# Layer 0's sum over 16 terms: a tree of additions in place of one strided reduction

## The chip, the core and the metric

The kernel runs on one core of a Trainium2 chip. The metric is the device time of one launch in microseconds. The core has five engines with a queue each, which run in parallel and wait for each other by semaphores: TensorE (PE, matrix products into PSUM; its weight loads are shown apart, as PEld), VectorE (DVE), ScalarE (ACT), GpSimd (POOL) and SyncE (SP); the last two mostly issue DMA transfers here.

## The reference

Four graph layers are applied in turn to x of 8 batches, 2048 nodes and 64 channels, with one 2048 x 2048 adjacency matrix `adj`. Each is a residual with a layer norm:

```python
x = _layernorm(x + L0(x, adj, embedding, weight, bias))   # graph convolution, weights per node
x = _layernorm(x + L1(x, adj, a))                         # attention
x = _layernorm(x + L2(x, adj, W, b))                      # mean over neighbours
x = _layernorm(x + L3(x, adj, iv, W1, b1, W2, b2))        # three message steps
```

Layer 0 is where the change lies. With K = 3 hops and D = 16 embedding entries per node:

```python
w = jnp.einsum('nd,dkio->nkio', embedding, weight)        # a weight matrix per node
As = [I, A, 2 A @ A - I]
x_g = jnp.einsum('knm,bmc->bnkc', jnp.stack(As), x)
out = jnp.einsum('bnki,nkio->bno', x_g, w) + embedding @ bias
```

The weight matrix of node n is a sum of 16 matrices, weighted with the 16 entries of its embedding. So the output of a node is a sum of 16 terms: x_g times matrix d, times embedding[n, d].

## The kernel before

**Tiling.** A tile has 128 nodes on the partitions; there are 16 node tiles. The 8 batches are taken as 4 pairs p, so that a tile of x is 128 nodes by 2 batches by 64 channels = 128x128, and `SX[p]` holds the 16 tiles of a pair. All data are fp32 (masks in DRAM are bf16). The adjacency matrix streams from DRAM in tiles of 512 KB (`a`), 6 of them in flight, through SP's queue in one fixed order (`order_of_a`, `fetch`).

**Layer 0.** `first_product` and `second_product` (the matmuls `acc`, line 1094) form A x and A (A x). Then `second_pass` makes, for each node tile, the products with all 16 matrices: 16 x 128 values per node come in two halves of 8 matrices, each half in a PSUM tile `yp` of 128 x 2 x 512 (line 601). `add_terms` takes a half from PSUM into the SBUF tile `terms` of 128 x 16 x 128, scaled with the node's embedding entry: 8 small ACT instructions per half (line 624). For pair 0 (`shared`) the second half is done by DVE instead, which adds its 8 terms onto the 8 of the first half (line 627), so that 8 terms are left. After the second half DVE sums what is in `terms` (16 terms, or 8 for pair 0) with one reduction into `added` (line 636) and adds that to the pair's tile `v` of `SX` (line 639). There are 64 such sums, 16 per pair: 16 of 8 terms and 48 of 16. When the four tiles of a chunk are done, `first_norm` and `layer_norm` follow (lines 482 to 510, 650).

**Layer 1.** `scores` finds each row's maximum with DVE (`junk`, line 732, 128x2048), and `weights` makes the attention weights `e` of 128x2048 in four steps: DVE adds a mask (line 810), ACT applies a leaky slope (line 818), DVE adds the negative maximum (line 823), ACT exponentiates (line 826). PE sums neighbours with them (`po`, line 837), and `finish` divides and adds.

**Layers 2 and 3.** They run on PE for pairs 0 and 1 as further sweeps over the adjacency matrix (also line 1094), with small products between them (`ps_u`, `ps_v`, lines 1029 and 1049). Pairs 2 and 3 are done jointly at the end (`joint_layer2`, line 1213, and `joint_layer3`, line 1300), with sums of adjacency quarters that are stored and read back (`s`, line 1173).

**What sets the order.** Every instruction's place in its engine's queue is fixed when the program is built. A planner (`Plan`) holds the generators of all this work as threads. Each thread names the engine that it wants next and what must be done before. The planner starts the thread that could begin earliest by its own clock, and `plan.run` advances that clock by a price that the code gives: `dve(n)` = n / 960 + 0.07 us, `act(n)` = n / 1220 + 0.14 us, and so on. Hence the price given for an instruction decides what is placed around it, on all engines, for the rest of the program; the adjacency sweeps (rank 1000) fill what is left of PE. Buffers are `Ring`s, which the planner also gives back at planned times; `terms` and the attention weights `e` share one of 4 buffers (`e_ring`).

For the sum of 16 terms the price before is `dve(2048) + dve(128) + 0.1` = 2.51 us, for that of 8 terms `dve(1024) + dve(128) + 0.1` = 1.44 us.

Of the kernel before, what the change touches and what calls it, by code (L numbers as in the profile page):

```python
# [12 lines left out]
ALU = mybir.AluOpType  # L13
AX = mybir.AxisListType
# [3 lines left out]
P = 128  # L18
# [10 lines left out]
D0 = 16  # L29
# [105 lines left out]
def dve(n, k=1):  # L135
    return k * (n / 960 + 0.07)
# [7 lines left out]
def resnorm_d4_kernel(  # L144
# [21 lines left out]
    nc = tc.nc  # L166
    plan = Plan()
# [28 lines left out]
    def tiny(shape, name, bufs=4):  # L196
        return wp.tile(shape, F32, tag=name, name=name, bufs=bufs)
# [7 lines left out]
    def batches(v):  # L205

        if len(v.shape) == 3:
            v = v.rearrange("p t n -> p (t n)")
        return v.rearrange("p (b c) -> p b c", c=C)
# [366 lines left out]
    def second_pass():  # L576

        for n in range(NPAIR * NCH):
# [4 lines left out]
            for j in range(TPC):  # L583
                t = c * TPC + j
                cs = slice(j * P, (j + 1) * P)
                for h in range(2):
                    hs = slice(h * CW, (h + 1) * CW)

                    ring = pp_ring
                    if p == 0 and po_ring.ready() < pp_ring.ready():  # L590
                        ring = po_ring
                    if h == 0 or ring.ready() > plan.free["PE"]:
                        yield "PE", [("xg", n + 1), got, ring, *([e_ring] if h == 0 else [])]
                    if h == 0:
                        terms = e_ring.take([P, D0, P], "terms")
                    yp, k = ring.take([P, 2, CW], "yp")

                    for k2 in (h, 1 - h):
                        for e in range(2):
                            rows = slice(e * C, (e + 1) * C) if k2 else slice(0, P)  # L600
                            nc.tensor.matmul(  # L601
                                yp[:, e, :],
                                lhsT=y2T[rows, cs] if k2 else xg[:, e, cs],
                                rhs=(wk2 if k2 else w01)[rows, hs],
                                start=(k2 == h),
                                stop=(k2 != h),
                            )
                    t_pe = plan.run("PE", 2.8, got)
                    plan.start((2, 2, 1, 1)[p], add_terms(p, c, t, h, yp, ring, k, terms, t_pe, left))
# [3 lines left out]
    def add_terms(p, c, t, h, yp, ring, k, terms, t_pe, left):  # L613

        shared = p == 0
        eng = "DVE" if shared and h else "ACT"
        yield eng, [t_pe, *([("terms", p, t)] if shared and h else [])]
        v = SX[p][:, t, :]
        for d in range(8):
            dd = h * 8 + d  # L620
            term = yp[:, :, d * C : (d + 1) * C]
            weight = emb_sb[:, t, dd : dd + 1]
            if eng == "ACT":
                nc.scalar.activation(batches(terms[0][:, dd, :]), term, AF.Copy, scale=weight)  # L624
            else:
                to = batches(terms[0][:, d, :])
                nc.vector.scalar_tensor_tensor(to, term, weight, to, ALU.mult, ALU.add)
        done = plan.run(eng, 8 * (0.255 if eng == "ACT" else 0.29), t_pe)
        ring.give(k, done)
        if h == 0:  # L630
            at["terms", p, t] = done
            return
        yield "DVE", [done]
        n = 8 if shared else D0
        added = tiny([P, P], "added", 1)
        nc.vector.tensor_reduce(  # L636
            added, terms[0][:, 0:n, :].rearrange("p d n -> p n d"), AX.X, ALU.add
        )
        nc.vector.tensor_tensor(v, v, added, ALU.add)
        done = plan.run("DVE", dve(n * P) + dve(P) + 0.1, done)  # L640
        e_ring.give(terms[1], done)
        left[0] -= 1
        if left[0] == 0:
            plan.start(2, first_norm(p, c, plan.free["DVE"] + plan.LAG))

    def first_norm(p, c, done):
        yield "DVE", [done]
        v = SX[p][:, tiles(c), :]
        v4 = v.rearrange("p t (e c) -> p t e c", c=C)
        nc.vector.tensor_tensor(  # L650
            v4, v4, eb[:, tiles(c), :].unsqueeze(2).to_broadcast([P, TPC, 2, C]), ALU.add
        )
        done = plan.run("DVE", dve(CW), done)
        done = yield from layer_norm(v, CW, done)
        at["n0", p, c] = done
        if all(("n0", p, i) in at for i in range(NCH)):
            at["x1", p] = max(at["n0", p, i] for i in range(NCH))
# [821 lines left out]
```

## Time and profile before

| | |
|---|---|
| median of 3 runs | 2170.16 us (2167.12 to 2171.02) |
| the profiled execution | 2166.21 us, span 2164.4 us |
| mean granted TensorE clock | 0.991 |
| busy: PE, DVE, ACT, POOL | 2081.7, 1552.5, 977.9, 213.6 us |
| sums of 16 terms (line 636) | 48, 3694 ns each, 177.3 us |
| sums of 8 terms (line 636) | 16, 1916 ns each, 30.7 us |
| additions onto x (line 639) | 64, 292 ns each, 18.7 us |
| first sum starts, last addition starts | 159.8 us, 1032.5 us |

The profile is of one execution. "Busy" is the time in which an engine has an instruction at work; a matmul's end is modelled, and matmuls overlap, so that PE's busy time overstates its load. An fp32 matmul of the program is two records in the trace. A wait is put down to the instruction that released it ("<-"), and the chain of waits follows the work that ended last back to its start. The times in a view are from the start of the span.

### The profile page before, as it was taken

The page shows a single profiled execution, that of the slowest core. Times are in us where ns is not written, and L with a number is a line of the kernel's source. Part 1 is how long each engine was busy: PE and PEld are TensorE (multiplying, and loading weights), DVE is VectorE, ACT ScalarE, POOL GpSimd, SP SyncE. Part 2 cuts the span into 40 slices and gives each one's busy share as a digit, 9 for nine tenths or more (in the row PEclk, how much of TensorE's full clock was granted, in tenths as well). Part 3 has the DMA queues.
Part 4 walks back from the last instruction along what each step waited for, and adds up shares of the span by engine and source line. Part 5 has one row for each costly group of instructions (what it writes and reads, how often), then busy time and mean ns, then how long its engine had stood idle before and what let it go on. Part 6 is the DMA issues. An engine that isn't in the chain of part 4 may idle for free.

```text
span 2164.4 us, 18851 instructions
## 1 busy us (share of the span) xinstructions
PE 2081.7 (96%) x6325; PEld 917.0 (42%) x6325; DVE 1552.5 (72%) x1727; ACT 977.9 (45%) x1799; POOL 213.6 (10%) x374
## 2 busy tenths in 40 slices
PE   8999999899999999999999999999999899999998
PEld 3444344334333343333444454443444344444444
DVE  2227648998899999879999979999697455020214
ACT  0025424367776556767653757516676022000002
POOL 2310000101010110110001011010010110000000
PEclk9999999999999999999999999999999999999999
DMA  9899835634353364543669778788776667878785
GB/s 300 268 335 345 290 105 197 218 102 127 90 170 125 116 211 160 180 156 122 232 239 371 232 250 323 250 320 300 247 252 234 231 249 271 283 249 283 252 290 187
DMA packets 208739, 495.84 MB, mean 229 GB/s; under 512 B 20275, under 2 KB 28595, under 8 KB 204531
## 3 DMA queue, kind: packets, MB, share of 16 engines
q1 hardware_dynamic: 165058, 347.62, 47.2%
q0 software_dynamic: 39360, 144.92, 19.6%
q10 hardware_dynamic: 4224, 2.10, 0.4%
q8 instruction: 50, 0.82, 0.1%
q14 instruction: 47, 0.38, 0.1%
HBM read 446.14 MB, written 46.33 MB: 228 GB/s over the span
## 4 chain that ended last, share of the span: by engine, by line
PE 40%; DVE 26%; issue 25%; ACT 5%; DMA 3%; POOL 1%; POOLq 0%; ACTq 0%; SPq 0%; DVEq 0%
PE acc L1094 26%; DVE added L636 8%; PE po L837 6%; DVE junk L732 5%; DVE e L810 5%; PE yp L601 5%; DVE e L823 4%; ACT terms L624 2%; DMA a<-in_adj_t 2%; ACT e L818 1%; PE ps_u L1029 1%; PE acc L1083 1%; POOL s L1175 1%; ACT e L826 1%; DVE ln_v L495 1%
## 5 line engine op out<-in xcount | busy, mean ns | idle before, releaser
L1094 PE MATMUL acc<-a,SX 128*128 128x512 f32 x1024 | 467.3, 600 | 10.9 <-DMA SX<-in_x 6.6
L1094 PE MATMUL acc<-a,SA 128*128 128x512 f32 x768 | 352.5, 600 | 6.9 <-DMA a<-in_adj_t 6.2
L818 ACT ACTIVATE e<-e,sv 128x1024 f32<-128x1024 f32 x256 | 279.5, 1147 | 162.8 <-DVE e L810 161.6
L823 DVE TENSOR_TENSOR e<-e,mb 128x2048 f32<-128x2048 f32 x128 | 290.7, 2284 | 12.7 <-ACT e L818 12.0
L1094 PEld LDWEIGHTS acc<-a,SX 128*128 128x128 f32 x1024 | 191.5, 192 | 253.4 <-issue 237.7
L732 DVE CUSTOM_DVE_ANT_0 junk<-s2b,mr 128x2048 bf16<-128x2048 f32 x128 | 292.5, 2285 | 1.8 <-DMA mr<-by_row 0.5
L810 DVE TENSOR_TENSOR e<-s1b,mk 128x2048 f32<-128x2048 f32 x128 | 289.3, 2283 | 0.9 <-DMA mk<-by_col 0.6
L826 ACT ACTIVATE e<-e 128x2048 f32<-128x2048 f32 x128 | 245.1, 1919 | 92.8 <-DVE e L823 92.4
L624 ACT ACTIVATE terms<-yp,emb_sb 128x128 f32<-128x128 f32 x896 | 242.2, 394 | 78.5 <-PE yp L601 78.3
L601 PE MATMUL yp<-SH,xgT 128*128 128x512 f32 x512 | 248.9, 611 | 7.2 <-ACT terms L624 3.6
L636 DVE TENSOR_REDUCE added<-terms 128x128 f32<-128x2048 f32 (+1 forms) x64 | 208.0, 3249 | 47.7 <-ACT terms L624 47.5
L837 PE MATMUL po<-e,SX 128*64 128x512 f32 x1024 | 235.9, 602 | 2.2 <-ACT e L826 2.2
L1094 PEld LDWEIGHTS acc<-a,SA 128*128 128x128 f32 x768 | 141.1, 191 | 177.7 <-issue 166.1
L1300 PE MATMUL acc<-a,t 128*128 128x512 f32 x384 | 168.7, 592 | 0.0
L601 PEld LDWEIGHTS yp<-SH,xgT 128*128 128x128 f32 x512 | 91.3, 190 | 150.2 <-issue 133.6
L601 PE MATMUL yp<-SH,y2T 64*128 64x512 f32 x512 | 131.1, 626 | 7.8 <-ACT y2T L543 6.1
L837 PEld LDWEIGHTS po<-e,SX 128*64 128x64 f32 x1024 | 67.9, 137 | 152.2 <-issue 136.0
L805 POOL DMA_DIRECT2D mk<-by_col x128 | 69.2, 542 | 612.0 <-DVE e L810 576.1
L1094 PE MATMUL acc<-a,SB 128*128 128x512 f32 x256 | 120.7, 601 | 0.0
L1300 PEld LDWEIGHTS acc<-a,t 128*128 128x128 f32 x384 | 72.0, 190 | 86.1 <-issue 86.1
L601 PEld LDWEIGHTS yp<-SH,y2T 64*128 64x128 f32 x512 | 43.7, 188 | 88.3 <-issue 73.4
L491 ACT ACTIVATE ln_sq<-SX 128x512 f32<-128x512 f32 x48 | 30.4, 633 | 96.8 <-DVE SX L484 45.1
(225 smaller groups left out, 1676.0 us busy)
## 6 DMA issues: line engine op xcount, KB each, us to landing
a<-in_adj_t SPq DMA_DIRECT2D x496, 512.0 KB, 5.5
a<-s SPq DMA_DIRECT2D x96, 512.0 KB, 4.5
mr<-by_row POOLq DMA_DIRECT2D x64, 512.0 KB, 5.7
mk<-by_col POOLq DMA_DIRECT2D x128, 256.0 KB, 5.3
an<-in_adj SPq DMA_DIRECT2D x16, 1024.0 KB, 10.6
s<-s POOLq DMA_DIRECT2D x32, 512.0 KB, 5.2
a<-a_plus_i SPq DMA_DIRECT2D x24, 512.0 KB, 5.5
by_col<-mk POOLq DMA_DIRECT2D x32, 256.0 KB, 5.9
```

The source lines that it names most:

```text
L601: nc.tensor.matmul(yp[:, e, :], lhsT=y2T[rows, cs] if k2 else xg[:, e, cs], rhs=(wk2 if k2 else w01)[rows, hs], start=(k2 == h), stop=(k2 ...
L624: nc.scalar.activation(batches(terms[0][:, dd, :]), term, AF.Copy, scale=weight)
L636: nc.vector.tensor_reduce(added, terms[0][:, 0:n, :].rearrange("p d n -> p n d"), AX.X, ALU.add)
L732: nc.vector.tensor_tensor_reduce(out=junk, in0=s2b[e][0], in1=masks[t][0], scale=1.0, scalar=LOWEST, op0=ALU.add, op1=ALU.max, accum_out=m ...
L805: nc.gpsimd.dma_start(mk, by_col[jt // 2][:, jt % 2, h * HALF : (h + 1) * HALF])
L810: nc.vector.tensor_tensor(e, s1b[0], mk.unsqueeze(1).to_broadcast([P, 2, HALF]), ALU.add)
L818: nc.scalar.activation(e[:, i, :], e[:, i, :], AF.Prelu, bias=sv[:, 2 + i, jt : jt + 1], alpha=ALPHA)
L823: nc.vector.tensor_tensor(e, e, mb[0], ALU.add)
L826: nc.scalar.activation(e, e, AF.Exp)
L837: nc.tensor.matmul(po[i * C : (i + 1) * C, f, :], lhsT=SX[p][:, t, i * C : (i + 1) * C], rhs=e[:, i, f * CW : (f + 1) * CW], start=(t == 0 ...
L1094: nc.tensor.matmul(pa, lhsT=source[:, m, :], rhs=t[:, i, :], start=(m == 0 and not seed), stop=(m == NT - 1),)
L1300: nc.tensor.matmul(pa, lhsT=B[:, 2 * r + b, :], rhs=at_[:, b, :], start=(r == 0 and b == 0 and not go_on), stop=(r == RQ - 1 and b == 1), ...
```

## The change

In `add_terms`, the reduction and the addition of its result become a tree of halvings in place, and two additions onto x. For 16 terms: terms 0 to 7 += terms 8 to 15 (1024 elements per partition), then 0 to 3 += 4 to 7 (512), then 0 and 1 += 2 and 3 (256), then x += term 0 and x += term 1 (128 each). For 8 terms the first step is left out. The reduction read its 16 values for one result 512 bytes apart; each addition reads and writes runs of consecutive elements. The planner's price is given as a number.

```diff
         yield "DVE", [done]
-        n = 8 if shared else D0
-        added = tiny([P, P], "added", 1)
-        nc.vector.tensor_reduce(
-            added, terms[0][:, 0:n, :].rearrange("p d n -> p n d"), AX.X, ALU.add
-        )
-        nc.vector.tensor_tensor(v, v, added, ALU.add)
-        done = plan.run("DVE", dve(n * P) + dve(P) + 0.1, done)
+        for half in (4, 2) if shared else (8, 4, 2):
+            a, b = (terms[0][:, i * half : (i + 1) * half, :] for i in range(2))
+            nc.vector.tensor_tensor(a, a, b, ALU.add)
+        for d in range(2):
+            nc.vector.tensor_tensor(v, v, terms[0][:, d, :], ALU.add)
+        done = plan.run("DVE", 1.75 if shared else 2.98, done)
         e_ring.give(terms[1], done)
```

The planner's price of the sum changes with it, from 2.51 to 2.98 us and from 1.44 to 1.75 us, so the places of other instructions change as well. The lines below this one move up by one (1094 becomes 1093, and so on).

## The prediction

> **What bounds the kernel now.** I read the page first (totals), then a table by stage, the chain of waits inside the stage that holds the sums, PE's waits there, and last the groups by form. The page's two totals:
>
> ```profile
> PE 2081.7 (96%) x6325; PEld 917.0 (42%) x6325; DVE 1552.5 (72%) x1727; ACT 977.9 (45%) x1799; POOL 213.6 (10%) x374
> ```
>
> Over the whole span DVE (72%) is no bound. By stage (columns: stretch, length, busy time with instruction counts of PE, PEld, DVE, ACT, POOL, granted clock, DMA share, GB/s) it is:
>
> ```profile
> 150.00:330.00 180.00, 175.86 (x516) 75.97 (x515) 113.56 (x263) 82.26 (x214) 14.99 (x26) 0.99 0.73 262
> 330.00:1050.00 720.00, 686.99 (x2074) 276.90 (x2074) 669.99 (x560) 463.43 (x1053) 69.99 (x127) 0.99 0.47 154
> 1050.00:1680.00 630.00, 619.21 (x2057) 276.32 (x2053) 577.92 (x561) 364.03 (x389) 69.05 (x124) 1.00 0.78 270
> ```
>
> Between 330 and 1050 us DVE is busy 93% and ACT 64%. All 48 full sums start between 330 and 1029 us; the 16 shorter ones (pair 0) lie in 150 to 330, where DVE is busy only 63%. The chain inside 330 to 1050, in its pieces around two sums (start, us, what):
>
> ```profile
> 993.48 3.62 DVE added L636
> 997.13 0.29 DVE SX L639
> 997.42 0.09 DVE ln_v L508
> ...
> 999.95 2.20 DVE e L810
> 1002.15 0.13 DVE rd L883
> 1002.30 0.69 DVE hp L885
> 1003.00 3.61 DVE added L636
> ```
>
> DVE instructions follow each other without a gap: here the chain is DVE's own queue, and L636 has the largest share of it (22.8% of this stage in the chain's summary). From 1050 us on the chain is PE (59% acc L1094, 21% po L837), from 1680 us on DVE is busy 156 of 484 us and PE runs the rest alone. So the sums sit on the binding engine, but PE is close behind. How close follows from PE's pitch when nothing holds it, again from pieces of the chain:
>
> ```profile
> 102.61 27.48 PE acc L1094 x64
> 283.39 11.10 PE yp L601 x32
> 1084.99 3.58 PE po L837 x16
> ```
>
> That is 0.429, 0.347 and 0.224 us a record. In 330 to 1050 the groups count 668 acc, 750 yp and 430 po records: 287 + 260 + 96 us, and 230 small ones at about 0.11 (transposes: 4 in some 0.42) make 25 more: 668 of 720 us. **PE idles about 52 us there**, although it shows 687 busy. PE's wait lists agree: what ends its weight loads' idle time other than "issue" adds up to about 57 us, led by
>
> ```profile
> PEld yp L601 <- ACT terms L624: 11.8, 11, 2.8
> PEld ps_xg L564 <- ACT terms L624: 10.0, 4, 5.1
> PEld yp L601 <- ACT y2T L543: 6.9, 1, 6.9
> PEld po L837 <- ACT e L826: 6.0, 7, 2.4
> ```
>
> and by the transposes behind mx. The same count gives 174 of 180 us for 150 to 330, and 607 of 630 for 1050 to 1680, where 23 us of wait are for DMA (a from in_adj_t).
>
> [...] The sum reads every term 512 bytes from the last, and takes 3694 ns for 2048 elements where plain 128x2048 adds take 2284[...]. [...] L636 to L639 above is a 0.03 us step. [...]
>
> **The change, part by part.** The prices:
>
> ```profile
> L636 DVE TENSOR_REDUCE added<-terms 128x128 f32<-128x2048 f32 x48 | 177.3, 3694 | 47.5 <-ACT terms L624 47.5
> L636 DVE TENSOR_REDUCE added<-terms 128x128 f32<-128x1024 f32 x16 | 30.7, 1916 | 0.2
> L639 DVE TENSOR_TENSOR SX<-SX,added 128x128 f32<-128x128 f32 x64 | 18.7, 292 | 2.2
> L1173 DVE TENSOR_TENSOR s<-a,s 128x1024 f32<-128x1024 f32 x8 | 9.8, 1223 | 1.4 <-DMA s<-s 1.2
> L510 DVE TENSOR_TENSOR SX<-SX,ln_r 128x512 f32<-128x512 f32 x48 | 33.2, 691 | 1.6
> ```
>
> 1. A full sum (48): out go 3.694 + 0.292 and one step of 0.03, 4.02 us. In come 1.223 + 0.690 + 0.424 + 2 x 0.292 and four steps of 0.03, 3.04 us. The 256-element add is not in the trace: the line through 128 and 512 gives 0.424; its ends are 0.29 and 0.69, so at worst 0.27 more each (13 us in all), at best 0.13 less (6 us). Saved: 0.98 x 48 = 47 us.
> 2. A short sum (16): out 1.916 + 0.292 + 0.03 = 2.24; in 0.690 + 0.424 + 0.584 + 0.09 = 1.79. Saved 0.45 x 16 = 7 us, beside a PE that has only 6 us of idle in that stage. I take 2 of the 7.
> 3. In place: the adds write over terms. L823 does so with 2048 elements and takes 2284 ns, L810 doesn't and takes 2283: nothing.
> 4. Buffers: terms is given back about 1 us sooner, added (32 KB) goes. PE waits behind this ring only through ACT; counted in the stall below, not again. No wait and no DMA is added: the first add waits for ACT's last scaling as the sum did, and SP's queue keeps its order. POOL's queue has the same transfers in another order.
> 5. The planner's price of a sum: 2.51 becomes 2.98 us (short: 1.44, 1.75). It schedules all engines by these, so orders move. Against the real 4.02 the old price ran 1.5 us early with every full sum; the new one is within 0.06. In the built orders, the last yp (L601) now has 22 more acc matmuls (0.859 us each, two records) and 16 more po matmuls (0.448) ahead of it: 26 us of work that PE has at hand while DVE sums. DVE has 11 more 2048-element operations ahead of its last sum, 24 us.
>
> DVE then: its last sum ended at 1032.8; 54 - 24 puts it at 1003 if its idle time stays. After it DVE has 11 operations less and ran 625 us without a break before, so its last mask addition would fall at about 1607 instead of 1662. PE: before the last yp, at 1020 us, it had 922 us of work at these pitches, 98 us of which were not work: 21 in the first 150 us, some 25 changes between kinds of matmul, and the rest stalls. Now it has 948. To be done by the 992 that DVE's 1003 asks for (the last yp led the last sum by 12 us), only 44 us could be lost, less than the first two items. So **DVE stops being the bound, and PE's own work becomes it.** The gain is not DVE's 54 but what goes of PE's 52 + 6 us of stalls. Two thirds is my choice: the DVE-driven part (mx, e and the lag of the plan) goes, the waits of yp for ACT's 8 scalings (L624 runs 2.2 us per half) stay. That is 38 us. After 1050 PE keeps its pitch; the DMA waits there I leave at 23, give or take 8.
>
> Sum: the profiled execution took 2166.2 us (span 2164.4); 2166.2 - 38 = 2128. The three runs' median, 2170.2, is 4 us above it; half of that is added: **2130 us**.
>
> **Rivals.**
> - PE floor (gain 8 to 26, about 2150): most of PE's stalls come from ACT, not from DVE. For: three of the four lines above name ACT. Against: ACT is busy 64% there and itself waits, 93.7 us for DVE L810 and 48.9 for L823 in this stage.
> - All of it (gain 49 to 62, about 2112): the corrected price removes nearly every stall, and some of the 23 us of DMA wait. For: 26 us of filler matmuls moved ahead. Against: PE would have to run at its pitch throughout.
> - No change (2166 to 2170): PE's 26 us of new filler delay yp by as much as DVE gains, so the stalls stay at 98 and only move. Against: filler is put where PE was to wait.
> - Slower, one mechanism: DMA in 1050 to 1680. SP's loads of a stay in order, POOL's loads of mr, s2b and mk shift against them. Two stretches already run that way (the chain shows a from in_adj_t for 15.1 us at 1154.6 and 13.9 at 1456.7). It decides when the waits grow from 23 by the 38 gained, to 61; at 75 the time is about 2182. For: the stage's DMA share is 0.78, 0.98 at 1150 to 1200. Against: 26 us of that stage's PE work move to a stage with 0.47.
> - That the tree isn't built is excluded: the order shows 48 adds of 1024, 64 of 512, 64 of 256 and 128 of 128 elements, and no reduction of terms.
>
> **How the numbers follow.** Likeliest 0.55 (gain 28 to 48, 2120 to 2140); PE floor 0.17; all of it 0.14; no change 0.04; slower 0.10. About 0.2%, 4 us, is what a measurement of this kernel can tell from none. Faster: 0.55 + 0.17 + 0.14 = 0.86. The range 2106 to 2160 leaves out slower, no change and slivers of the two neighbours, 0.2; it holds the 256-element add's bounds (+13, -6).
>
> **What would show it.** Right: L636 with forms of 1222, about 690 and 424 ns; the last sum near 1005; PE's non-issue waits in 330 to 1050 near 20 us instead of 57; joint products (L1213) starting near 1637 instead of 1675, and the rest shifted as a block. Wrong: an add far from its price, stalls that keep their size, or a DMA wait above 40 us after 1050.

## The result, and the profile after

The median falls from 2168.64 us (4 runs) to **2134.81 us** (4 runs, 2133.99 to 2137.42): a ratio of 0.985, 95% interval 0.9838 to 0.9862, or 33.8 us less. The profiled execution took 2133.99 us; its span is 2132.2 us, 32.2 us less than before.

The page's totals after (busy time, share of the span, instructions):

```profile
PE 2067.3 (97%) x6325; PEld 914.9 (43%) x6325; DVE 1496.4 (70%) x1908; ACT 974.9 (46%) x1794; POOL 213.0 (10%) x374
```

DVE's busy time fell by 56.1 us. These are the groups by form, where there were one reduction and one addition (columns as before: busy us, mean ns, idle before):

```profile
L636 DVE TENSOR_TENSOR terms<-terms 128x1024 f32<-128x1024 f32 x48 | 58.6, 1220 | 38.2 <-ACT terms L624 38.2
L636 DVE TENSOR_TENSOR terms<-terms 128x512 f32<-128x512 f32 x64 | 44.2, 691 | 1.8
L638 DVE TENSOR_TENSOR SX<-SX,terms 128x128 f32<-128x128 f32 x128 | 37.4, 292 | 4.4
L636 DVE TENSOR_TENSOR terms<-terms 128x256 f32<-128x256 f32 x64 | 27.2, 425 | 2.2
```

The four durations are within 3 ns of the prices that the prediction took, with 425 ns for the 256-element addition, which the trace before did not have. PE's waits between 330 and 1000 us, all of them (us in total, times, longest):

```profile
PE ps_y L531 <- ACT y1T L358: 2.4, 2, 1.5
PE ps_xg L564 <- ACT terms L624: 0.4, 1, 0.4
PE ps_rows L784 <- DVE sv L358: 0.2, 1, 0.2
```

3.0 us are left; before, that stretch has 30.0 us of them. But a new place has turned up. The table by stretch, the columns as in the prediction, with the cuts laid at the last yp (1002), the first product of layer 3 (1052) and the start of the joint layers (1652):

```profile
330.00:1002.00 672.00, 668.99 (x2053) 272.96 (x2052) 616.85 (x690) 457.45 (x1027) 70.45 (x128) 1.00 0.50 163
1002.00:1052.00 50.00, 34.91 (x129) 15.95 (x128) 47.52 (x70) 33.38 (x57) 3.22 (x6) 0.86 0.39 125
1052.00:1652.00 600.00, 585.12 (x1928) 260.66 (x1926) 535.28 (x506) 332.76 (x351) 64.45 (x116) 1.00 0.79 270
1652.00:2132.00 480.00, 461.33 (x1331) 224.16 (x1329) 156.26 (x276) 55.78 (x125) 23.86 (x41) 0.99 0.77 262
```

In the 50 us after the last yp PE is busy 35. Its waits there:

```profile
PE ps_vT L1015 <- DVE v L1007: 7.4, 1, 7.4
PE ps_emb L981 <- DVE SB L990: 3.5, 2, 2.9
PE acc L1093 <- ACT z L945: 3.1, 1, 3.1
PE po L836 <- ACT e L825: 1.1, 1, 1.1
```

This is pair 0's way from layer 2 to layer 3 (`layer2_tail`, `start_chunk`), which the planner admits only after pair 3's last sum and norm; I call it the handover. Before, the same way has hardly a gap, with PE busy 50.8 of 53 us:

```profile
1020.00:1073.00 53.00, 50.83 (x182) 23.54 (x181) 52.28 (x62) 32.98 (x55) 3.75 (x7) 1.00 0.67 223
```

**Where the time went, as a balance of PE.** With the prediction's pitches (records times 0.429, 0.347 or 0.224 us, small ones 0.11) each stretch's idle time is its length less the work of its records. A pitch is rounded, so that a figure is good to about 1 us. Every kernel below has the same PE records, so its span is 2038.5 us of work plus that idle time by construction (within 1 us); what the table tells is where the idle time lies. Stretches: to 330 us; to the last yp; to the first product of layer 3; to the first joint product (L1213 before, L1212 after); to the end.

| us of PE idle | to 330 | to last yp | to layer 3 | to joint | to end | sum | span |
|---|---|---|---|---|---|---|---|
| before | 22.2 | 49.7 | 2.8 | 19.3 | 31.7 | 125.7 | 2164.4 |
| after | 18.8 | 9.5 | 19.1 | 24.3 | 22.0 | 93.7 | 2132.2 |
| e1, tree, old price | 16.9 | 12.7 | -0.1 | 21.1 | 32.0 | 82.6 | 2121.6 |
| e2, reduction, new price | 24.6 | 47.5 | 21.7 | 23.5 | 20.9 | 138.2 | 2176.1 |
| e3, reduction, true price | 19.8 | 13.5 | 13.8 | 47.9 | 31.9 | 126.9 | 2165.4 |
| e4, no halvings, new price | 20.5 | 7.9 | 16.9 | 25.0 | 22.6 | 92.9 | 2131.7 |
| e6, no halvings, old price | 21.2 | 6.1 | 0.0 | 18.9 | 31.7 | 77.9 | 2116.9 |
| e7, adjacent terms, old price | 21.9 | 6.3 | 0.0 | 20.9 | 32.5 | 81.6 | 2120.2 |
| e9, two chunks later, new price | 19.1 | 17.4 | 1.3 | 22.9 | 31.1 | 91.8 | 2131.0 |

The change takes 40 us of idle time out before the last yp, puts 16 in after it, 5 in up to the joint layers, and takes 10 out at the end.

Not all of this "idle" time is waiting. The clock column shows stretches in which TensorE was granted half its clock, and there a matmul takes twice its pitch: before, four records of 0.429 us start in the 3.4 us from 1684.7, 0.85 us each. The first line below is of the kernel before, the second of the changed one:

```profile
1684.70:1688.10 3.40, 3.40 (x6) 1.34 (x5) 2.57 (x6) 0.63 (x1) 0.00 (x0) 0.50 0.00 0
1035.10:1048.80 13.70, 6.26 (x20) 3.49 (x22) 13.29 (x29) 6.56 (x17) 0.00 (x0) 0.50 0.00 0
```

What such a stretch adds is, by estimate, the work of the records that start in it. Between 330 us and the last yp the trace before has five of them, 20.4 us long in all, each beginning some 3 to 5 us after the start of a wait of PE of about 3 to 6 us; their records come to 10 us at pitch. The changed kernel has none there. So of the 40 us, some 27 are waits that went (30.0 us to 3.0) and 10 are the clock; 3 are left over. In the handover of the changed kernel the listed waits are 15.1 us and the half clock adds 3, together 18 of the 19.1.

### The profile page after: what moved, and what is told of

The parts are those of the page before. It is cut to its first block, busy times and chain, and to the rows that moved or that the text cites. A ratio compares the mean times of both kernels' runs of the same rounds, so it can differ in the third digit from the quotient of the medians.

```text
span 2132.2 us, 19037 instructions
## 1 busy us (share of the span) xinstructions
PE 2067.3 (97%) x6325; PEld 914.9 (43%) x6325; DVE 1496.4 (70%) x1908; ACT 974.9 (46%) x1794; POOL 213.0 (10%) x374
## 5 line engine op out<-in xcount | busy, mean ns | idle before, releaser
L1093 PEld LDWEIGHTS acc<-a,SX 128*128 128x128 f32 x1024 | 190.3, 191 | 242.2 <-issue 229.6
L636 DVE TENSOR_TENSOR terms<-terms 128x512 f32<-128x512 f32 (+1 forms) x176 | 130.0, 738 | 42.2 <-ACT terms L624 38.2
L1093 PEld LDWEIGHTS acc<-a,SB 128*128 128x128 f32 x256 | 47.2, 190 | 57.3 <-issue 57.3
## 6 DMA issues: line engine op xcount, KB each, us to landing
mk<-by_col POOLq DMA_DIRECT2D x128, 256.0 KB, 5.0
by_col<-mk POOLq DMA_DIRECT2D x32, 256.0 KB, 5.8
```

The lines of the kernel that those rows point to most:

```text
L636: nc.vector.tensor_tensor(a, a, b, ALU.add)
L1093: nc.tensor.matmul(pa, lhsT=source[:, m, :], rhs=t[:, i, :], start=(m == 0 and not seed), stop=(m == NT - 1),)
```

## The experiments

Ratios are to the kernel before, which ran beside each. Where nothing else is said, the order is that of the kernel whose prices are used: for e1, e2 and e4 every queue but DVE's holds the same instructions in the same order as in the kernel with those prices.

**Operation or price?** The diff holds two changes: what DVE does, and what the planner thinks that it costs.

e1 is the tree with the old prices:

```diff
-        done = plan.run("DVE", 1.75 if shared else 2.98, done)
+        done = plan.run("DVE", dve((8 if shared else D0) * P) + dve(P) + 0.1, done)
```

> The tree with the planner's old prices (2.51 and 1.44 us), so that every queue outside the sum itself has the order of the kernel before. Theory A (DVE's time): the 54 us of DVE work that the tree saves cut PE's stalls by themselves; the time falls by 20 to 30 us of the 34, to about 2140 to 2148. Rival B (the price): the gain comes from the order that the corrected price makes, and with the old order PE stalls as before; the time stays at 2160 or more.

Measured: 2124.88 us, ratio 0.9814 (0.9801 to 0.9828). Theory A was right and too cautious: the operation alone gains 40 us, more than the whole change.

e2, the reduction with the new prices (the same edit the other way, in the kernel before):

> The strided reduction with the changed kernel's prices (2.98 and 1.75 us), so that every queue outside the sum has the order of the changed kernel. Theory A: DVE still carries the 54 us, so at most 10 us are gained, 2158 to 2168, and PE's stalls between 330 and 1030 us stay above 40 us. Rival B: the order does it, about 2140.

Measured: 2176.17 us, ratio 1.0048 (1.0036 to 1.0061): slower than before. Neither theory had that. The new price costs 10 us (0.0048 x 2165) with the reduction, and 8 (0.985 less 0.9814) to 10 (the medians) with the tree. The balance says where: 22 us of idle time in the handover, as in the changed kernel and not in the old order, and 11 less at the end.

e3, the reduction with its measured price:

```diff
-        done = plan.run("DVE", dve(n * P) + dve(P) + 0.1, done)
+        done = plan.run("DVE", 2.24 if shared else 4.02, done)
```

> The strided reduction with its measured price (4.02 and 2.24 us). If the harm was a plan that ran ahead of DVE (rival B), the time falls to about 2140 with DVE's work unchanged. Theory A: DVE is the bound of the stage from 330 to 1030 us and a true price cannot shorten it; 2155 to 2168.

Measured: 2165.74 us, ratio 0.9997 (0.9988 to 1.0005). A true price moves PE's idle time (13.5 us before the last yp instead of 49.7, 47.9 up to the joint layers instead of 19.3) and removes none of it. Rival B is out.

**Is DVE's sum still on the bound after the change?** e4 and e6 leave the three halving steps out, in the new and in the old order, so that most terms are missing from their results:

```diff
-        for half in (4, 2) if shared else (8, 4, 2):
-            a, b = (terms[0][:, i * half : (i + 1) * half, :] for i in range(2))
-            nc.vector.tensor_tensor(a, a, b, ALU.add)
```

> The changed kernel without the halving additions: only terms 0 and 1 are added onto x, so 14 of the 16 terms (6 of 8 for pair 0) are left out of the result. Price and orders are those of the changed kernel; DVE does 48 x 2.34 + 16 x 1.11 = 130 us less. If PE's own work is the bound after the change, as the prediction has it, this is worth at most 12 us more: 2122 to 2135. If DVE is still the bound of the stage from 330 to 1010 us, it is worth 30 us or more: 2105 or less.

> The tree with the old prices, without the halving additions: only terms 0 and 1 are added onto x (14 of 16 terms left out, 6 of 8 for pair 0). DVE has 130 us less to do than with the tree and the same order. If PE's own work bounds the kernel in this order too, at most 10 us are gained on the tree with the old prices (2124.9): 2115 to 2125. If DVE still held PE up between 330 and 1000 us, 2100 or less.

Measured: 2130.77 us, ratio 0.984 (0.9827 to 0.9854), 2 to 4 us less than the changed kernel by ratio and median; and 2119.42 us, ratio 0.9779 (0.9765 to 0.9792), 5 to 8 us less than e1. With 130 us less to do on DVE, a sixteenth of that or less arrives. Up to the last yp PE is down to 8 and 6 us of idle time, and the changed kernel has 9.5. So after the change PE's own work is the bound of that stage, and the sums are off it. The handover is another matter: PE still idles 16.9 us there in e4, with no halvings at all.

**Why does the new order cost?** In the order with the old price 538 acc and 200 po matmuls stand ahead of the last yp, with the new price 560 and 216. They are no extra work: they are missing afterwards. From the last yp to layer 3's first product runs a chain of some 50 us in these orders (ACT's scalings, the sum, pair 3's norm, ps_emb, pair 0's norm, ps_vT, ps_u). To cover it, PE has 38 acc and 24 po matmuls = 43 us in the old order, but 16 and 24 = 24 us in the new one.

My first form of this was that the position of the last chunk matters. e5 moves it behind the second of the ps_emb:

```diff
             need=lambda q: [("x2", p)],
+            before=lambda c: [("emb", 0, 1)] if p == 0 and c == NCH - 1 else [],
...
         done = plan.run("PE", mm(P, TPC), done)
         yt_ring.give(kz, done)
+        at["emb", p, c] = done
```

> The changed kernel, tree and prices as they are, but the last chunk of pair 0's layer 2 product (16 matmuls, 14 us of PE) is placed between the second and the third of the small products that follow it (ps_emb), instead of before the first. Theory C (handover): the order that the new price makes uses up all adjacency matmuls before the handover from pair 0's layer 2 to layer 3, where PE then waits some 20 us between 1000 and 1060 us for DVE's layer norms; with the chunk kept for that place most of this goes, 2120 to 2128. Rival D: the new order's loss is spread over the whole stage from 1000 to 1640 us and one chunk doesn't matter, 2131 to 2138.

Measured: 2138.57 us, ratio 0.9867 (0.9851 to 0.9884): theory C failed in this form. PE's waits between 1000 and 1080 us:

```profile
PE po L836 <- ACT e L825: 14.6, 3, 5.9
```

The wait only went to the po matmuls that now came first, and 23.9 us at half clock, with 6 us of work in them, came with it. 24 us of work stay 24 us wherever they stand.

e8 does the same with the old prices:

> The tree with the old prices and the held chunk of e5. The old order already has 14 adjacency matmuls left at the handover, so theory C expects no more than 3 us either way from the tree with the old prices, 2122 to 2128. Should it be well below, the held chunk does something other than cover the handover.

Measured: 2131.53 us, ratio 0.9834 (0.982 to 0.9847), 4 to 7 us slower than e1 where 3 were allowed. The cover was there already (less than 1 us of idle time in the chain); the balance of its profiled execution has 4 us more on the way to the joint layers, and 5 more before 330 us, where the profiled executions differ by as much without a reason in the change (16.9 to 24.6). Holding a chunk back costs something of its own; what, I have not shown.

e9 tests the amount instead. The planner may place pair 0's last two layer 2 chunks only after the latest group of yp that it has placed; in the order that results 32 acc and 24 po matmuls follow the last yp:

```diff
             need=lambda q: [("x2", p)],
+            before=lambda c: ["last_yp"] if p == 0 and c >= 2 else [],
...
             yt_ring.give(ky, t_pe)
             xg_ring.give(kx, t_pe)
+            at["last_yp"] = t_pe
```

> The changed kernel with its prices, but the last two chunks of pair 0's layer 2 product may not be placed before the last yp. Theory E (independent work after the last yp): from the last yp to the first product of layer 3 a chain of about 50 us runs through ACT, DVE's sum and norms and back (1002 to 1052 us in the changed kernel, 978 to 1028 with the old prices). PE has 16 acc and 24 po matmuls = 24 us to fill it with in the changed order, 38 and 24 = 43 us in the old one. Here it has 32 and 24 = 38 us, so 10 to 14 us of the stall go: 2120 to 2128. Rival D (the loss lies elsewhere in the new order): 2131 to 2138.

Measured: 2132.82 us, ratio 0.9843 (0.9828 to 0.9857), which cannot be told from the changed kernel's 0.985. That independent work fills the handover is shown: the idle time in the chain fell from 19.1 to 1.3 us. A gain is not: 8 us came back before the last yp (PE had to wait for an attention tile, 5.5 us, where it had had these chunks, and 2 us of work ran at half clock behind that wait) and 9 at the end. The end is worth a look. PE's waits at the start of the joint layers, 1627 to 1720 us of e1:

```profile
PE po L1212 <- DVE SX L510: 4.2, 1, 4.2
PE ps_vT L1015 <- DVE SX L510: 3.1, 2, 1.6
PE acc L1212 <- DMA a<-in_adj_t: 2.6, 1, 2.6
```

The wait for pair 3's last norm (SX L510) is there in the kernel before (4.2), in e1 and in e9 (4.2), and not in the changed kernel. Where PE lost 19 us after the last yp, DVE went on in the meantime, and pair 3 was ready when PE came to it: DVE's last mask addition ended 32 us before the first joint product in the changed kernel, 17 us before it in the kernel before, in e1 and in e9. That is my reading of why about half of what the new order loses at the handover is given back at the end. The listed waits explain some 6 of these 10 us. The other 4 are the clock: e1 has two stretches at half clock there, whose records come to 4 us at pitch, and the changed kernel has none before 2124 us, when its matmuls are done.

```profile
1638.80:1645.60 6.80, 4.55 (x6) 1.97 (x7) 5.01 (x14) 1.25 (x4) 0.00 (x0) 0.50 0.00 0
1676.40:1679.80 3.40, 3.40 (x6) 1.33 (x5) 1.57 (x3) 0.00 (x0) 1.06 (x2) 0.50 1.03 411
```

e10, a price between the two (2.75 and 1.60):

> The tree with a price between the two (2.75 us, short 1.60). Its order leaves 28 acc and 16 po matmuls = 31 us between the last yp and the first product of layer 3. Theory E puts it between the changed kernel's 24 us (2134.8) and the old order's 43 us (2124.9): 2126 to 2133. If the nearness of the price to the real 3.04 us mattered, it would be slower than with 2.98 us.

Measured: 2127.64 us, ratio 0.9816 (0.9798 to 0.9834), with runs from 2123.26 to 2131.84. Its idle time in the chain is 7.8 us, between 0 and 19 as its 31 us of cover are between 43 and 24. The price nearer to the real one (2.98 us) is not the better one: what counts is the order that happens to come of it.

**Was the reduction slow, or its reads?** e7 keeps one reduction and the old prices, and turns the layout of `terms` round. This leaves the order of the kernel before:

```diff
-                        terms = e_ring.take([P, D0, P], "terms")
+                        terms = e_ring.take([P, P, D0], "terms")
...
-                nc.scalar.activation(batches(terms[0][:, dd, :]), term, AF.Copy, scale=weight)
+                nc.scalar.activation(batches(terms[0][:, :, dd]), term, AF.Copy, scale=weight)
...
-            added, terms[0][:, 0:n, :].rearrange("p d n -> p n d"), AX.X, ALU.add
+            added, terms[0][:, :, 0:n], AX.X, ALU.add
```

(DVE's own line for pair 0 changes like ACT's.)

> One reduction as before, with the old prices and so the old order, but terms are stored with the 16 terms of one result next to each other, so that the reduction reads consecutive elements, and ACT writes each term with a step of 64 bytes. If the reduction was slow because of its reads 512 bytes apart, it takes 2.2 to 2.4 us instead of 3.69, which is less than the tree's 3.04 with its additions. If the reduction itself is slow, it stays at 3.5 us or more. ACT's scaling (0.39 us) may become longer with its strided writes; at 0.5 us or less the kernel takes 2115 to 2128, at 0.7 us ACT binds the stage and it is 2170 or more.

Measured: 2120.83 us, ratio 0.978 (0.9765 to 0.9795). The groups of e7:

```profile
L624 ACT ACTIVATE terms<-yp,emb_sb 128x128 f32<-128x128 f32 x896 | 256.0, 494 | 116.0 <-PE yp L601 115.8
L636 DVE TENSOR_REDUCE added<-terms 128x128 f32<-128x2048 f32 x48 | 109.5, 2281 | 52.4 <-ACT terms L624 50.8 <-ACT ln_r L501 1.2
L627 DVE SCALAR_TENSOR_TENSOR terms<-yp,emb_sb,terms 128x128 f32<-128x128 f32 x128 | 45.3, 438 | 46.6 <-PE yp L601 46.6
```

The reduction takes 2281 ns where it took 3694: it was the reads 512 bytes apart. The price goes to the writers: a scaling on ACT lasts 494 ns instead of 394, DVE's line for pair 0 438 instead of 343. But ACT's instructions overlap (896 times 494 ns would be 443 us), so that ACT's busy time for the group grows only from 242.2 to 256.0 us, and ACT has room (busy for 46% of e7's span, 45% before). This is the fastest version that computes everything: 14 to 15 us below the changed kernel, 48 below the one before (0.022 x 2167.2).

e11 adds e9's idea to it, with three chunks (`c >= 1`):

> The version of e7 (one reduction over adjacent terms, old prices) with the last three chunks of pair 0's layer 2 product not placed before the last yp: 48 acc and 16 po matmuls = 48 us for the chain of 50. Theory E: the old order had 43 us and stalled little, so at most 5 us are left, 2114 to 2122 against 2120.8. If it is slower than 2124, moving chunks late delays layer 3 by more than the cover gives.

Measured: 2133.12 us, ratio 0.9842 (0.9828 to 0.9856): 12 us slower than e7. With 0.0 us of idle in the chain there was nothing to win. The way to the joint layers has 35.1 us of idle instead of 20.9.

**The short sums.** e12 has the tree and the old prices for the 48 full sums alone:

> The tree with the old prices and order for the 48 full sums alone; the 16 short sums of pair 0 keep the reduction. The prediction priced the short sums at 7 us of DVE work and took 2 of it. Expected 2125 to 2129 against 2124.9 with both; if the short sums were on the bound like the full ones, 2131 or more.

Measured: 2126.03 us, ratio 0.9812 (0.9797 to 0.9827), against e1's 0.9814. The 7 us that the tree saves on pair 0's sums bring nothing that can be measured.

## Why the prediction was right, and where it was not

- **DVE's saving** (47 + 7 us): right. The prices were within 3 ns each, and DVE's busy time, which doesn't count the steps between instructions (0.03 us from L636 to L639 before), fell by 56.1 us.
- **The short sums** (2 of 7 us taken): e12 shows no effect, but its interval is too wide to tell none from 2 us. The reason given (PE has 6 us of idle there) is not contradicted.
- **DVE stops being the bound and PE's work becomes it**: shown by e4 and e6 for the stage up to the last yp. This is why 54 us of DVE work were not 54 us of time. One sum of the working is off: PE's work ahead of the last yp is 948 us before the change, not 922 (1019.5 less 22.2 and 49.7), apparently because the 25 us for changes of kind were added to stalls that already held them. After the change it is 974, which leaves 18 us to lose by 992 and not 44; the conclusion only gets firmer. The last yp started at 1002 us, and the last sum ended at 1013 where 1003 was forecast.
- **The gain is PE's stalls, two thirds of 58 us**: the term was mis-sized. Between 330 us and the last yp more than two thirds went: 49.7 us of idle time became 9.5, with the waits of yp for ACT's scalings among them, which I expected to stay. ACT had been waiting for DVE in its turn: up to the last yp its attention steps waited 132.0 us for DVE's mask addition (91.8) and its addition of the negative maximum (40.2), and after the change 71.9 (50.8 and 21.1). About 10 of the 40 us were matmuls at half clock, a term that the prediction doesn't have. The sign that I named, weight-load waits near 20 us instead of 57 between 330 and 1050 us, came out at 37: 19 before the last yp and 18 in the handover.
- **The planner's price** (part 5): this is the step that failed. I read the 22 acc and 16 po matmuls that move ahead of the last yp as 26 us of work "at hand while DVE sums", a help, and did not ask what would be missing behind it. e1 and e2 show that the new order costs 8 to 10 us, with the tree and without it. The rival "no change" had the filler's harm in view, at the wrong place and size.
- **The way after 1050 us** ("PE keeps its pitch"): wrong in three places: +16 us at the handover, which begins a little before 1050, +5 up to the joint layers and -10 at the end.
- **The sum**: 38 us for the gain against 33.8 measured. That it is so near is luck in part: a stage gain larger than expected (40 us of idle time) and a loss through the order that was not expected at all nearly came to the expected figure. The joint layers began at 1652 us and not at 1637, which is where the page contradicts the prediction.
- **DMA as the slower side**: not seen. PE waits for `a` 10.1 us between 1000 and 1640 us, 8.3 before; its weight loads 15.9, 14.9 before. The 23 us of the prediction equal 8.3 and 14.9 added, which are the same waits seen twice.

## What to carry to other kernels

Here the gain of shorter work on an engine with a full queue was bounded by the idle time of the engine behind it: with 54 us less on DVE, 37 (e1) to 40 of the 49.7 us went that PE idled up to the last yp, and with 130 us less again (e4, e6) no more than 7. In such a case count the second engine's work by its undisturbed pitch and keep a balance of its idle time by stage, before and after, with the granted clock beside it. Where a planner's price is changed along with an operation, time the two apart: here the operation gains 40 us, and the more truthful price takes 8 to 10 of them back, by using up independent matmuls that a later dependent chain needed as cover. And before a strided reduction is replaced by more instructions, see whether its producer can write what it reads side by side: that took this one from 3694 to 2281 ns.

## What the runs showed that was not expected

ACT writing a 128x128 tile with a step of 64 bytes takes 494 ns instead of 394 for one instruction, but little more in a row: the group's busy time grew by 6%, from 242.2 to 256.0 us. About a quarter of the idle time that the change removed before the last yp (10 of 40 us) was not waiting but matmuls at half clock behind the waits. And the order of static queues alone, with nearly the same instructions on every engine, is worth as much as 130 us of work on DVE once PE is the bound: 8 to 10 us between e1 and the changed kernel, against 2 to 8 us for leaving out the halvings.
